# Sums brought to the nodes by products with a stored permutation, in a four-layer graph kernel

## The chip, the cores and the metric

The kernel runs on one core of one Trainium2 chip, in one launch. The metric is device time in microseconds; lower is better. A core has a matrix engine (PE, with its weight loads shown as PEld), a vector engine (DVE), a scalar engine (ACT), a general engine (POOL), a sync engine (SP) that issues transfers, and 16 DMA engines that all queues share. Each engine works through its own queue in order; between engines, semaphores order the work.

## The reference

`x` is 16 graphs of 1024 nodes with 64 features, `adj` their symmetric 0/1 adjacency, `nodemask` is all true. Four layers follow each other; each ends in a residual addition and a layer normalisation over the features. Layers 0 and 3 are the same function with other weights:

```python
adj_d = _dilate_adj(adj, mask)              # drops some edges of nodes with over 10 neighbours
agg   = sum over (tau, w) in ((.25,.25), (.5,.5), (.75,.25)):
            w * interpolated quantile tau, per node and feature, of x over the node's neighbours
out   = x + agg
y     = (relu(out @ W1 + b1) @ W2 + b2) * mask
x     = layernorm(x + y)
```

Layer 1 is `adj @ (x @ W) + b`, layer 2 is `gelu(((softmax(x W1 W2' x') + adj) @ x) @ G)`, both with the same ending. The quantiles need a sort of each node's neighbours for each of the 64 features, and that is most of the work.

## The kernel before

**Batches and layers.** For each of the 16 graphs (batches) there are two sorting layers, numbered l = 0 (reference layer 0) and l = 1 (reference layer 3). The kernel runs 32 of them in an order made by `layers`: batches 0, 1 and 2 of l = 0 first, then in turn one of l = 1 and one of l = 0, with l = 1 two batches behind, and the rest of l = 1 at the end. A layer's place in this order is n. From n = 2 to 28 the even n are l = 0 and the odd ones l = 1; n = 29, 30 and 31 are l = 1.

**A graph's lists (`graph`, called by `graph_stream`).** For each batch, `neighbours` and `both_ways` compute the thinned adjacency `near`, `order` sorts the nodes by degree and stores the order as a 0/1 matrix times 2048 in float16, `perm` (128 x 8 x 1024; its memory is shared with `nbt` by the tag "turned"), and `lists` (line 1104) turns it into lists: `hidx`, the neighbour numbers of the 128 nodes with the longest lists (the hubs), `idx`, those of the other 896 nodes, in seven tiles of 128 nodes with at most 22, 16, 13, 11, 10, 9 and 8 slots, and the weights `wt` and `hwt`. It also makes, by small products with `perm`, `node` and `hnode` (lines 1182 to 1192): for each place in the order, the number of the node that stands there. Up to five batches' lists are kept (`KEPT`), and graph b waits for the end of layer 1 of batch b - 5.

**Gathers (`fetch_stream`, line 1289, all on POOL).** A layer first gathers hub rows: 60 indirect DMAs into `hrows`, a ring of 8 buffers, each free again when `turn_stream` has transposed it into `cols`. Then come the rows of the short lists: 22 into `rows0`, 29 into `rows1`, 38 into `rows2`, one buffer each. Each indirect DMA fetches one row of 64 features per partition from a DRAM table of the nodes' features.

**Sorting.** `turn_stream` (PE transposes, ACT copies) brings the hub rows into `cols`. `sort_stream` (line 1379, DVE) sorts the long lists there (`long_lists`, which end in `tot`), and then runs a sorting network over each of the three groups of short rows. `turn_stream` turns `tot` into `hagg` (64 x 2 x 64). `pick_stream` (line 1393) weights the sorted rows on ACT and adds them in PSUM on PE, which gives `agg[0..2]` (128 nodes x 1, 2 and 4 tiles x 64). `hagg` and `agg` are the aggregates in the degree order, not in the order of the nodes.

**Bringing the sums home.** `put` (line 1240) is an indirect DMA on POOL that writes one tile of aggregates to the rows of a DRAM table `sums` named by `node` or `hnode`. A layer has two for the hubs (`put_hub`) and seven for the short tiles (`put_short`). For n up to `SOON` = 2 they come before the next layer's gathers (`put_all`); later, the two hub puts come after the next layer's 60 hub gathers, and the 1, 2 and 4 others ahead of its `rows0`, `rows1` and `rows2` gathers. Since `rows1` and `rows2` have one buffer each, each of those gathers needs the sort of the layer before in that group to be done, and the `put` waits for just that ("sorted").

**The middle (`middle_stream`).** For each n in order `last_step` (line 1529) reads `sums` back as `ag`, adds the features, transposes (8 times 128 columns), and applies the two dense layers and the normalisation. For l = 0 it goes on with reference layers 1 and 2 (`spread_layer`, `attention_layer`), both of which multiply by the adjacency with `by_adj` (line 1560): 16 loads of 256 KB into `at`, which has three buffers, each followed by a product of 512 columns. The result `x3` is the table of the layer l = 1 of that batch.

**What sets the order.** The streams are generators. `give_out` (line 211) goes through them with estimated costs and due times, always takes the step that could start first (on a tie, the earlier stream: graph, turn, pick, weight, middle, sort, fetch), and so writes out one fixed order for each engine's queue, the queues of SP and ACT for DMAs among them. `Wait(event)` holds a stream back until another stream has given out the step that sets the event; `.after(t)` adds t ns to the estimated readiness of a step.

Of the kernel before, what the change touches and what calls it, by code (L numbers as in the profile page):

```python
# [41 lines left out]
LAG = 2  # L42
KEPT = LAG + 3
SPARE = max([CH * HC] + [64 * n * s for _, n, s in TILE_GROUPS])
SOON = 2
HROWS = 8


# [735 lines left out]
def listed_path(ctx: ExitStack, tc: tile.TileContext, x, adj, nodemask,  # L784
# [48 lines left out]
    V.tensor_scalar(tie_up, tie, 1.0 / (4 * N), None, ALU.add)  # L833
    key_row = const.tile([1, N], F16, name="key_row")
    G.iota(key_row, pattern=[[1, N]], base=1 - 2048, channel_multiplier=0, allow_small_or_imprecise_dtypes=True)
    node16 = iota([P, NT], F16, [[P, NT]], cm=1, name="node16")

    numbers = const.tile([P, NT, 2 * CH - 1], F16, name="numbers")
    V.memset(numbers, 0.0)
# [242 lines left out]
    def order(op, pso, deg, perm):  # L1082
# [18 lines left out]
        for t in range(NT):  # L1101
            yield V.tensor_scalar(perm[:, t], place, rank[:, t:t + 1], 2048.0, ALU.is_equal, ALU.mult)

    def lists(lp, psl, b, near, perm, deg, k):

        k.idx = kp.tile([P, 7, MOST], U32, name="idx")
        k.hidx = kp.tile([P, 2, NG], U32, name="hidx")
        k.node = kp.tile([P, NT], U32, name="node")
        k.hnode = kp.tile([64, 2], U32, name="hnode")
        k.wt = kp.tile([P, 7, MOST], F32, name="wt")  # L1110
        k.hwt = dram.tile([P, CH, 2 * HC], F16, name="hwt", bufs=KEPT)
        dn = lp.tile([P, 2, NT], F16, name="dn")
        yield V.tensor_copy(dn[:, 0], deg)
        yield V.tensor_copy(dn[:, 1], node16)


        pt = psl.tile([P, NT, P], F32, name="two")
# [58 lines left out]
            yield V.tensor_scalar(k.idx[:, g - 1, :cap], top[:, :cap], 0.0, None, ALU.max)  # L1176
        events.add(("idx", b))

        pd = psl.tile([P, NT, 2], F32, name="one")
        for g in range(NT):  # L1180
            for t in range(NT):
                yield T.matmul(pd[:, g, :], perm[:, t, g * P:(g + 1) * P], dn[:, :, t],
                         start=(t == 0), stop=(t == NT - 1))
        dg = lp.tile([P, NT], F32, name="dg")
        yield V.tensor_scalar(dg, pd[:, :, 0], 1.0 / 2048, None, ALU.mult)
        yield V.tensor_scalar(k.node, pd[:, :, 1], 1.0 / 2048, None, ALU.mult)
        ph = psl.tile([64, 2], F32, name="one")
        for h in range(2):
            for t in range(NT):
                yield T.matmul(ph[:, h:h + 1], perm[:, t, h * 64:(h + 1) * 64], dn[:, 1, t:t + 1],  # L1190
                         start=(t == 0), stop=(t == NT - 1))
        yield V.tensor_scalar(k.hnode, ph, 1.0 / 2048, None, ALU.mult)
        more = lp.tile([P, NT], F32, name="more")
        yield V.tensor_tensor(more, dg, caps, ALU.subtract)
        most = lp.tile([P, 1], F32, name="most")
# [22 lines left out]
        for r in range(4):  # L1218
            hd = lp.tile([P, 8, 2 * HC], F16, name="hd")
            for c0, _, n, k0, chunks, by_list in HUB_RUNS:  # L1220
                cols = slice(c0, c0 + n * chunks)
                names, dim = ("(l k)", 2) if by_list else ("(k l)", 3)
                shape = [P, 8, n, chunks] if by_list else [P, 8, chunks, n]
                yield V.tensor_tensor(hd[:, :, cols].rearrange(f"p s {names} -> p s {names[1:-1]}", k=chunks),
                                      hw[:, k0 * CH:(k0 + chunks) * CH].rearrange("p (k s) -> p s k", k=chunks)
                                      [:, 8 * r:8 * r + 8].unsqueeze(dim).to_broadcast(shape),
                                      my_list[:, cols].rearrange(f"p {names} -> p {names[1:-1]}", k=chunks)
                                      .unsqueeze(1).to_broadcast(shape), ALU.mult)
            ho = lp.tile([P, 8, 2 * HC], F16, name="ho")
            for q in range(2):  # L1230
                pw = psl.tile([P, 8 * HC], F32, name="one")
                yield T.matmul(pw, halves, hd[:, 4 * q:4 * q + 4].rearrange("p s c -> p (s c)"), start=True, stop=True)
                yield A.copy(ho[:, 4 * q:4 * q + 4].rearrange("p s c -> p (s c)"), pw)
            yield A.dma_start(k.hwt[:, 8 * r:8 * r + 8, :], ho)

    def fetched(table, dst, rows):
        return G.indirect_dma_start(out=dst, out_offset=None, in_=table[:, :],
                                    in_offset=bass.IndirectOffsetOnAxis(ap=rows, axis=0))

    def put(sums, rows, src):  # L1240
        return G.indirect_dma_start(out=sums[:, :], out_offset=bass.IndirectOffsetOnAxis(ap=rows, axis=0),
                                    in_=src, in_offset=None)

    def slots_ap(buf, place, f, width):

# [22 lines left out]
        if b >= LAG:  # L1268
            layers.append((1, b - LAG))

    def put_hub(n, k):
        yield Wait("hagg", n)
        yield Wait("sums", n)
        for h in range(2):
            yield put(k.sums, k.hnode[:, h:h + 1], k.hagg[:, h])

    def put_short(n, k, q):
        t0, ntiles, _ = TILE_GROUPS[q]
        yield Wait("sorted", n, q)
        for t in range(ntiles):  # L1280
            yield put(k.sums, k.node[:, t0 + t:t0 + t + 1], k.agg[q][:, t])

    def put_all(n, k):
        yield from put_hub(n, k)
        for q in range(3):
            yield from put_short(n, k, q)
        events.add(("put", n))

    def fetch_stream():
        for n, (l, b) in enumerate(layers):  # L1290
            k = batches[b]
            yield Wait("hidx", b) if l == 0 else Wait("x3", b)
            table = tables[l][b % (2 + l * (LAG - 1))]
            k.hrows = [None] * NG
            last = batches[layers[n - 1][1]] if n else None
            early = n <= SOON
            if n and early:
                yield from put_all(n - 1, last)
            for g in range(NG):
                m = n * NG + g - HROWS  # L1300
                if m >= 0:
                    yield Wait("turned", m // NG, m % NG // 4)
                rows = qp.tile([P, 2, C], F32, name="hrows", bufs=HROWS)
                e = min(P, (2 * HC - g * GC) * CH)
                for h in range(2):
                    yield fetched(table, rows[:e, h, :], k.hidx[:e, h, g:g + 1])
                k.hrows[g] = rows
                events.add(("h", n, g))
            if n and not early:
                yield from put_hub(n - 1, last)  # L1310
            yield Wait("idx", b)
            for q, (t0, ntiles, places) in enumerate(TILE_GROUPS):
                if n and not early:
                    yield from put_short(n - 1, last, q)
                rows = qp.tile([P, places, ntiles, C], F32, name=f"rows{q}")
                for t in range(ntiles):
                    for s in range(TILE_CAPS[t0 - 1 + t]):
                        yield fetched(table, rows[:, s, t, :], k.idx[:, t0 - 1 + t, s:s + 1])
                k.rows[l, q] = rows
                events.add(("rows", n, q))  # L1320
            if n and not early:
                events.add(("put", n - 1))
        yield from put_all(n, batches[layers[-1][1]])

    def turn_stream():
        for n, (l, b) in enumerate(layers):
            k = batches[b]
# [51 lines left out]
    def sort_stream():  # L1379
        for n, (l, b) in enumerate(layers):  # L1380
            k = batches[b]
            yield Wait("cols", n, 0)
            if n > 1:
                yield Wait("put", n - 2)
            k.tot = qp.tile([P, 64], F32, name="tot", bufs=2)
            yield from long_lists(n, k)
            events.add(("hubdone", n))
            for q, (_, ntiles, places) in enumerate(TILE_GROUPS):
                yield Wait("rows", n, q)
                yield from network((k.rows[l, q], spare((places, ntiles, C))), plans[q], C)  # L1390
                events.add(("net", n, q))

    def pick_stream():

        for n, (l, b) in enumerate(layers):
            k = batches[b]
            if n > 1:
                yield Wait("put", n - 2)
            k.agg = []
            for q, (t0, ntiles, _) in enumerate(TILE_GROUPS):  # L1400
                yield Wait("net", n, q)
# [127 lines left out]
    def last_step(n, l, b, k):  # L1529
# [1 line left out]
        w1, b1, w2, b2 = ends[l]  # L1531
        xn = features("xn")
        yield D.dma_start(xn, by_part(x[b] if l == 0 else k.x3[1:, :]))
        yield Wait("put", n)
        ag = features("ag")
        yield D.dma_start(ag, by_part(k.sums)).after(8000)
        yield V.tensor_add(ag, ag, xn).after(5000)
        py = one([P, NT, C])
        yield T.matmul(py, ones_row, b2.unsqueeze(1).to_broadcast([1, NT, C]), start=True, stop=False)
        for h in range(NH):  # L1540
            ts = range(h * (HALF // P), (h + 1) * (HALF // P))
            pt = one([C, HALF])
            for t in ts:
                yield T.transpose(pt[:, t % (HALF // P) * P:(t % (HALF // P) + 1) * P], ag[:, t, :], ident)
            ot = mp.tile([C, HALF], F32, name="ot")
            yield A.copy(ot, pt)
            ph = one([H, HALF])
# [10 lines left out]
        return (yield from layernorm(z, ag, features("y")))  # L1558

    def by_adj(k, xn):  # L1560

# [88 lines left out]
    def middle_stream():  # L1650
        for n, (l, b) in enumerate(layers):
            k = batches[b]
            k.sums = dram.tile([N, C], F32, name="sums", bufs=2)
            events.add(("sums", n))
# [70 lines left out]
```

## Time and profile before

| | us |
|---|---|
| median of three runs | 8264.22 |
| lowest and highest of the three | 8253.03, 8267.44 |
| the profiled execution | 8260.65 |
| its span, first to last instruction | 8258.9 |
| mean granted PE clock, as a share of full speed | 0.739 |

The span is what the profile divides into shares. Its page gives busy time per engine; time in which an engine's queue issues a DMA or waits counts as idle, also on POOL, where each indirect DMA is shown as an instruction of about a microsecond. A line of a group reads: engine, operation, tile written <- tiles read, count, then busy time and mean duration in ns, then the idle time just before these instructions and what ended most of it. Starts of the steady part, read off POOL's first hub gather of each layer: layer 7 starts at 2145.7 us, layer 9 at 2632.3, layer 11 at 3117.2, and so on to layer 27 at 7000.7; layers 28 to 31 start at 7246.6, 7478.0, 7705.5 and 7932.8. Layer 3 starts at 1101.0, layers 0, 1 and 2 at 188.8, 520.0 and 883.8. The last hub gather's layer ends its gathers at 8165.0.

### The profile page before, as it was taken

Reading aid. Unit: us, or ns where it says so; the run is one execution under the profiler, and the core shown is the slowest. Engines: PE = TensorE matmul, PEld = TensorE weight load, DVE = VectorE, ACT = ScalarE, POOL = GpSimd, SP = SyncE. Lnnn points to the kernel's source line nnn. Section 1 sums busy time; section 2 is a strip of 40 time slices with the busy share of each in tenths; the row PEclk is TensorE's granted clock in tenths of the full one; section 3 lists DMA queues with packets and bytes.
Section 4 is the critical chain, followed back from the end, with each engine's and each line's share of the span. In section 5 each row is a group of like instructions: output and inputs, shape, how many; then the busy total and the mean of one; then the engine's idle time right before and its main releaser. Section 6 shows DMA issues by size and latency. Waiting matters only on the chain. (4 is left out here: it accounts for less than half of the span.)

```text
span 8258.9 us, 83245 instructions
## 1 busy us (share of the span) xinstructions
PE 5314.9 (64%) x24947; PEld 2777.2 (34%) x24947; DVE 6878.5 (83%) x14791; ACT 2726.7 (33%) x7346; POOL 5640.8 (68%) x5087
## 2 busy tenths in 40 slices
PE   6568786847657576675857667585766758272542
PEld 4243433333333333333333333333333333131221
DVE  2769688778889888888988888898888889889685
ACT  3333433233242424324242432424233242221221
POOL 0635567657676776767777676777777777777774
PEclk8779877768778686877868677686877769565655
DMA  1322424232332323223232322323242232232311
GB/s 48 70 64 57 95 44 98 44 72 51 68 74 54 79 58 82 50 56 82 57 74 58 86 53 51 80 62 75 51 93 52 52 77 65 33 68 36 66 32 21
DMA packets 761595, 513.79 MB, mean 62 GB/s; under 512 B 458672, under 2 KB 600112, under 8 KB 760880
## 3 DMA queue, kind: packets, MB, share of 16 engines
q1 hardware_dynamic: 457008, 261.89, 13.3%
q0 software_dynamic: 161792, 163.90, 12.5%
q10 hardware_dynamic: 142336, 82.59, 3.3%
q8 instruction: 202, 3.31, 0.2%
q14 instruction: 257, 2.11, 0.1%
HBM read 408.64 MB, written 103.55 MB: 62 GB/s over the span
## 5 line engine op out<-in xcount | busy, mean ns | idle before, releaser
L180 POOL DMA_INDIRECT rows<-table,idx x2848 | 3247.0, 1140 | 868.0 <-issue 840.3
L180 POOL DMA_INDIRECT hrows<-table,hidx x1920 | 2054.8, 1070 | 1069.3 <-issue 457.2
L180 DVE TENSOR_TENSOR spare<-cols 128x528 f32<-128x528 f32 (+11 forms) x1632 | 1058.9, 675 | 74.6 <-ACT cols L180 49.1
L180 DVE TENSOR_TENSOR cols<-spare 128x528 f32<-128x528 f32 (+11 forms) x1664 | 1073.2, 681 | 14.8
L180 PE MATMUL turned<-ident,hrows 128*128 128x128 f32 x960 | 348.2, 394 | 936.8 <-DMA hrows<-table,hidx 663.1
L180 PE MATMUL picked<-rows,ident 128*128 128x64 f32 (+2 forms) x2496 | 676.0, 388 | 399.8 <-ACT rows L180 398.9
L180 PEld LDWEIGHTS picked<-rows,ident 128*128 128x128 f32 x2496 | 500.8, 259 | 557.9 <-ACT rows L180 483.3
L180 POOL DMA_INDIRECT sums<-agg,node x224 | 261.3, 1166 | 559.1 <-DMA sums<-agg,node 175.3
L180 ACT ACTIVATE rows<-rows,wt 128x64 f32<-128x64 f32 x2272 | 608.4, 340 | 104.2 <-DVE rows L180 104.2
L180 DVE TENSOR_TENSOR spare<-rows 128x64 f32<-128x64 f32 (+8 forms) x1056 | 542.4, 543 | 80.9 <-DMA hrows<-table,hidx 25.1
L180 PE MATMUL two<-run,nbt 128*128 128x512 f16 (+3 forms) x1536 | 426.4, 452 | 238.0 <-ACT v L180 238.0
L180 PEld LDWEIGHTS turned<-ident,hrows 128*128 128x128 f32 x960 | 169.7, 185 | 1197.2 <-issue 713.3
L180 PE MATMUL pi<-hot,numbers 128*32 128x236 f16 x4096 | 521.1, 273 | 70.1 <-DVE hot L180 66.1
L180 PEld LDWEIGHTS <-nbt 128*128 128x128 f16 x3584 | 310.6, 115 | 670.8 <-issue 610.7
L180 PE MATMUL two<-near,perm 128*128 128x512 f16 x1792 | 507.0, 434 | 0.0
L180 PEld LDWEIGHTS <-numbers 128*32 128x32 f16 x4096 | 382.4, 99 | 335.9 <-issue 291.1
L180 DVE TENSOR_TENSOR spare<-spare 128x944 f32<-128x944 f32 (+11 forms) x672 | 451.2, 671 | 19.1
L180 DVE TENSOR_TENSOR rows<-spare 128x512 f32<-128x512 f32 (+9 forms) x896 | 459.2, 538 | 1.3
L180 ACT COPY cols<-turned 128x512 f32<-128x512 f32 (+3 forms) x288 | 149.2, 529 | 870.9 <-PE turned L180 867.9
L180 PE MATMUL one<-xt,wt 64*128 64x512 f32 x512 | 356.7, 821 | 62.8 <-DVE top L180 62.7
L180 DVE TENSOR_TENSOR spare<-cols,spare 128x472 f32<-128x472 f32 (+2 forms) x704 | 380.9, 541 | 14.7
L180 DVE TENSOR_TENSOR rows<-rows,spare 128x64 f32<-128x64 f32 (+4 forms) x1120 | 364.8, 331 | 19.2
(238 smaller groups left out, 10048.0 us busy)
## 6 DMA issues: line engine op xcount, KB each, us to landing
at<-adjt SPq DMA_DIRECT2D x512, 256.0 KB
a<-in_adj_dram SPq DMA_DIRECT2D x128, 512.0 KB
adjt<-at ACTq DMA_DIRECT2D x128, 512.0 KB
rows<-table,idx POOLq DMA_INDIRECT x2848
hrows<-table,hidx POOLq DMA_INDIRECT x1920
hw<-hwt SPq DMA_DIRECT2D x64, 472.0 KB
hwt<-ho ACTq DMA_DIRECT2D x64, 236.0 KB
ag<-sums SPq DMA_DIRECT2D x32, 256.0 KB
```

Of the source, the lines that this page charges most:

```text
L180: return Step(lambda: f(*args, **kw), self.engine, cost, late, reads, writes, "dma" in name)
```

## The change

The puts, `node`, `hnode`, `sums` and `SOON` are gone. `lists` ends in a new function, `turned_order`: it transposes `perm` back on PE (64 blocks of 128 x 128 in float16), scales it to 0/1 in float32 on ACT, and stores it from ACT's queue as `back` in DRAM, 4 MB a graph. In `last_step` the sums are not read back: for each half of 512 nodes the aggregates are multiplied by the matching rows of `back` (two products with `hagg`, seven with `agg`), which adds every aggregate to its node's column in one PSUM tile, transposed as the dense layer needs it; each of the nine products has its own load into `at`, the tile with three buffers that `by_adj` uses too. The features are added by four more products with the identity, in place of DVE's addition and the transposes. `rows0` gets a second buffer, so that its gathers need the sort of the layer before the last one only. `tot`, `hagg` and `agg`, which waited for the event "put" of layer n - 2, wait for "used", which is set when the products of that layer have been given out.

```diff
+    def turned_order(lp, psl, perm, k):
+
+        k.back = dram.tile([NH, N, HALF], F32, name="back", bufs=KEPT)
+        for g in range(NT):
+            pb = psl.tile([P, NT, P], F16, name="one")
+            for t in range(NT):
+                yield T.transpose(pb[:, t, :], perm[:, t, g * P:(g + 1) * P], ident16)
+            back = lp.tile([P, N], F32, name="rest", bufs=2)
+            yield A.activation(back, pb.rearrange("p t n -> p (t n)"), AF.Copy, scale=1.0 / 2048)
+            yield A.dma_start(k.back[:, g * P:(g + 1) * P, :].rearrange("h r n -> r h n"),
+                              back.rearrange("r (h n) -> r h n", h=NH))
...
     def lists(lp, psl, b, near, perm, deg, k):
-        k.node = kp.tile([P, NT], U32, name="node")
-        k.hnode = kp.tile([64, 2], U32, name="hnode")
...
-        yield V.tensor_scalar(k.node, pd[:, :, 1], 1.0 / 2048, None, ALU.mult)
-        ph = psl.tile([64, 2], F32, name="one")
-        for h in range(2):
-            for t in range(NT):
-                yield T.matmul(ph[:, h:h + 1], perm[:, t, h * 64:(h + 1) * 64], dn[:, 1, t:t + 1],
-                         start=(t == 0), stop=(t == NT - 1))
-        yield V.tensor_scalar(k.hnode, ph, 1.0 / 2048, None, ALU.mult)
...
+        yield from turned_order(lp, psl, perm, k)
...
     def fetch_stream():
...
-            if n and early:
-                yield from put_all(n - 1, last)
...
-            if n and not early:
-                yield from put_hub(n - 1, last)
             yield Wait("idx", b)
             for q, (t0, ntiles, places) in enumerate(TILE_GROUPS):
-                if n and not early:
-                    yield from put_short(n - 1, last, q)
-                rows = qp.tile([P, places, ntiles, C], F32, name=f"rows{q}")
+                if n > (q == 0):
+                    yield Wait("sorted", n - 1 - (q == 0), q)
+                rows = qp.tile([P, places, ntiles, C], F32, name=f"rows{q}", bufs=1 + (q == 0))
...
     (sort_stream and pick_stream)
-                yield Wait("put", n - 2)
+                yield Wait("used", n - 2)
...
     def last_step(n, l, b, k):
-        yield Wait("put", n)
-        ag = features("ag")
-        yield D.dma_start(ag, by_part(k.sums)).after(8000)
-        yield V.tensor_add(ag, ag, xn).after(5000)
+        yield Wait("hagg", n)
+        for q in range(3):
+            yield Wait("sorted", n, q)
...
             pt = one([C, HALF])
+            for g in range(NT + 1):
+                at = mp.tile([P, HALF], F32, name="at", bufs=3)
+                if g < 2:
+                    yield D.dma_start(at[:64], k.back[h, g * 64:(g + 1) * 64, :])
+                    yield T.matmul(pt, k.hagg[:, g], at[:64], start=(g == 0), stop=False)
+                else:
+                    q = sum(t0 < g for t0, _, _ in TILE_GROUPS) - 1
+                    yield D.dma_start(at, k.back[h, (g - 1) * P:g * P, :])
+                    yield T.matmul(pt, k.agg[q][:, g - 1 - TILE_GROUPS[q][0]], at, start=False, stop=False)
             for t in ts:
-                yield T.transpose(pt[:, t % (HALF // P) * P:(t % (HALF // P) + 1) * P], ag[:, t, :], ident)
+                c0 = t % (HALF // P) * P
+                yield T.matmul(pt[:, c0:c0 + P], xn[:, t, :], ident, start=False, stop=(t == ts[-1]))
+            if h == NH - 1:
+                events.add(("used", n))
```

More of the change, by code (lines that the diff above doesn't have):

```diff
@@ L44 @@
 SPARE = max([CH * HC] + [64 * n * s for _, n, s in TILE_GROUPS])
-SOON = 2
 HROWS = 8
@@ L835, in listed_path @@
     G.iota(key_row, pattern=[[1, N]], base=1 - 2048, channel_multiplier=0, allow_small_or_imprecise_dtypes=True)
-    node16 = iota([P, NT], F16, [[P, NT]], cm=1, name="node16")
     numbers = const.tile([P, NT, 2 * CH - 1], F16, name="numbers")
@@ L1107, in lists @@
         k.hidx = kp.tile([P, 2, NG], U32, name="hidx")
-        k.node = kp.tile([P, NT], U32, name="node")
-        k.hnode = kp.tile([64, 2], U32, name="hnode")
         k.wt = kp.tile([P, 7, MOST], F32, name="wt")
         k.hwt = dram.tile([P, CH, 2 * HC], F16, name="hwt", bufs=KEPT)
-        dn = lp.tile([P, 2, NT], F16, name="dn")
-        yield V.tensor_copy(dn[:, 0], deg)
-        yield V.tensor_copy(dn[:, 1], node16)
+        d16 = lp.tile([P, NT], F16, name="d16")
+        yield V.tensor_copy(d16, deg)
         pt = psl.tile([P, NT, P], F32, name="two")
@@ L1177, in lists @@
         events.add(("idx", b))
-        pd = psl.tile([P, NT, 2], F32, name="one")
+        pd = psl.tile([P, NT], F32, name="one")
         for g in range(NT):
             for t in range(NT):
-                yield T.matmul(pd[:, g, :], perm[:, t, g * P:(g + 1) * P], dn[:, :, t],
+                yield T.matmul(pd[:, g:g + 1], perm[:, t, g * P:(g + 1) * P], d16[:, t:t + 1],
                          start=(t == 0), stop=(t == NT - 1))
         dg = lp.tile([P, NT], F32, name="dg")
-        yield V.tensor_scalar(dg, pd[:, :, 0], 1.0 / 2048, None, ALU.mult)
-        yield V.tensor_scalar(k.node, pd[:, :, 1], 1.0 / 2048, None, ALU.mult)
-        ph = psl.tile([64, 2], F32, name="one")
-        for h in range(2):
-            for t in range(NT):
-                yield T.matmul(ph[:, h:h + 1], perm[:, t, h * 64:(h + 1) * 64], dn[:, 1, t:t + 1],
-                         start=(t == 0), stop=(t == NT - 1))
-        yield V.tensor_scalar(k.hnode, ph, 1.0 / 2048, None, ALU.mult)
+        yield V.tensor_scalar(dg, pd, 1.0 / 2048, None, ALU.mult)
         more = lp.tile([P, NT], F32, name="more")
@@ L1238, in fetched @@
                                     in_offset=bass.IndirectOffsetOnAxis(ap=rows, axis=0))
-    def put(sums, rows, src):
-        return G.indirect_dma_start(out=sums[:, :], out_offset=bass.IndirectOffsetOnAxis(ap=rows, axis=0),
-                                    in_=src, in_offset=None)
     def slots_ap(buf, place, f, width):
@@ L1269, in listed_path @@
             layers.append((1, b - LAG))
[L1271 to L1287, printed above, removed]
     def fetch_stream():
@@ L1294, in fetch_stream @@
             k.hrows = [None] * NG
-            last = batches[layers[n - 1][1]] if n else None
-            early = n <= SOON
-            if n and early:
-                yield from put_all(n - 1, last)
             for g in range(NG):
@@ L1320, in fetch_stream @@
                 events.add(("rows", n, q))
-            if n and not early:
-                events.add(("put", n - 1))
-        yield from put_all(n, batches[layers[-1][1]])
     def turn_stream():
@@ L1397, in pick_stream @@
             if n > 1:
-                yield Wait("put", n - 2)
+                yield Wait("used", n - 2)
             k.agg = []
@@ L1557, in last_step @@
         yield V.tensor_add(z, z, xn).after(6000)
-        return (yield from layernorm(z, ag, features("y")))
+        return (yield from layernorm(z, features("ag"), features("y")))
     def by_adj(k, xn):
@@ L1652, in middle_stream @@
             k = batches[b]
-            k.sums = dram.tile([N, C], F32, name="sums", bufs=2)
-            events.add(("sums", n))
             y = yield from last_step(n, l, b, k)
```

## The prediction

> **What bounds the kernel now.** Every instruction carries line 180, the helper that records it, so I go by tiles. I read four views in this order: the page's busy sums, the busy times in windows cut at the first hub gather of every second layer, the POOL groups and timeline inside those windows, and then the waits of DVE and PE.
>
> ```profile
> PE 5314.9 (64%) x24947; PEld 2777.2 (34%) x24947; DVE 6878.5 (83%) x14791; ACT 2726.7 (33%) x7346; POOL 5640.8 (68%) x5087
> ```
> ```profile
> 4573.80:5061.60 487.80, 332.83 (x1573) 172.73 (x1572) 430.73 (x928) 172.66 (x464) 354.34 (x316) 0.76 0.31 66
> 5061.60:5546.60 485.00, 330.51 (x1557) 174.11 (x1557) 427.71 (x922) 169.15 (x458) 354.36 (x316) 0.75 0.32 66
> ...
> 7478.00:7705.50 227.50, 57.81 (x187) 40.12 (x187) 190.89 (x399) 41.84 (x158) 171.86 (x159) 0.50 0.22 34
> ```
> (Window and its length, busy us and instructions of PE, PEld, DVE, ACT, POOL, then granted clock, DMA share, GB/s.) By the busy sums DVE is the bound and POOL has a third to spare. The windows correct this. From 2145.7 to 7000.7 us there are ten equal pairs of layers (one of each kind, with one graph), 485.5 us each; DVE is busy 428 of them, PE 329, POOL 353 in 316 or 317 transfers. But a POOL transfer is not 1.12 us: each is followed by 0.30 us of issue.
>
> ```profile
> 4674.33 0.92 POOL L180 DMA_INDIRECT hrows<-table,hidx  x1 [0.30 <-issue]
> 4675.55 0.92 POOL L180 DMA_INDIRECT sums<-hagg,hnode  x1 [0.30 <-ACT ag L180]
> 4677.91 1.00 POOL L180 DMA_INDIRECT sums<-hagg,hnode  x1 [1.44 <-DMA sums<-hagg,hnode]
> 4680.79 0.97 POOL L180 DMA_INDIRECT sums<-agg,node  x1 [1.88 <-DVE rows L180]
> 4682.07 1.53 POOL L180 DMA_INDIRECT rows<-table,idx  x1 [0.30 <-issue]
> ```
> The POOL groups between 2145 and 7000 us (busy, mean ns | idle before):
> ```profile
> L180 POOL DMA_INDIRECT rows<-table,idx x1781 | 2034.7, 1142 | 542.8 <-issue 533.6 <-DMA rows<-table,idx 5.2 <-PE pi L180 2.4
> L180 POOL DMA_INDIRECT hrows<-table,hidx x1200 | 1289.9, 1075 | 519.7 <-issue 285.0 <-PE turned L180 161.3 <-DMA hrows<-table,hidx 53.3
> L180 POOL DMA_INDIRECT sums<-agg,node x140 | 167.6, 1197 | 214.8 <-DMA sums<-agg,node 106.0 <-DVE spare L180 25.6 <-DVE nb L180 21.6
> L180 POOL DMA_INDIRECT sums<-hagg,hnode x40 | 42.2, 1055 | 44.7 <-DMA sums<-hagg,hnode 38.6 <-issue 3.0 <-ACT ag L180 2.7
> ```
> Busy and idle of these four lines add to 4856 of 4855 us: POOL's queue is never without work, and only 161 us of it waits for another engine (the hub gathers for a free place). So **POOL is the bound**, and the puts hold it 167.6 + 42.2 + 214.8 + 44.7 = 469 us in ten pairs, 47 a pair, half of it because one put waits for the one before it to land. DVE waits next to never for gathered rows (2.8 us in the ten pairs); the bound reaches it through PE, whose queue stands behind turns that wait for hub rows (waits of PE, then of DVE, 4573 to 5061 us):
>
> ```profile
> PE turned L180 <- DMA hrows<-table,hidx: 43.0, 27, 6.7
> PE turned L180 <- ACT cols L180: 19.5, 3, 12.1
> ...
> PE turned L180 <- DVE tot L180: 12.2, 2, 6.5
> ```
> ```profile
> DVE deg L180 <- ACT near L180: 10.9, 1, 10.9
> DVE z L180 <- ACT z L180: 9.5, 2, 8.8
> ```
>
> **What it removes.** All 288 puts, the `sums` table with its write and read, and on DVE one 0.68 us addition a layer and three copies of about 0.16 us a graph. POOL's own work for a pair falls to (4856 - 469 - 161) / 10 = 422 us. DVE's falls to 428 - 1.4 - 0.5 = 426, and its gaps under 150 ns (3204 in the ten pairs, 112 us by the time stamps) make that 437. So **DVE's 437 is the next floor**, before any wait.
>
> **What it adds to PE.** Per layer, 18 products of 512 columns in float32. The nearest row is the adjacency product, which loads its operand the same way: two passes, 1.07 us.
> ```profile
> 3422.99 1.07 PE L180 MATMUL po<-at,y 128*64 128x512 f32 x2
> ```
> 36 x 1.07 = 38.5 us a pair. Eight transposes a layer become products of the same 128 columns in two passes (+0.11 us each, +2 a pair); 64 f16 transposes a graph at 108.1 us / 1024 (the row one<-ident,nb) are 6.8; 16 tiny products go (-0.5). Together +47: PE goes from 329 to 376 of the pair. Bounds: the passes start 0.43 us apart, so 31 us at least for the 36; 36 x 1.07 plus the mean load pace below at most.
>
> [...]
>
> **What it adds to the queues.** SP: 18 loads a layer (4.2 MB) through three `at` buffers. The adjacency product runs the same loop at 16 products in 3417.5 to 3460.2 us, 2.4 us a load, so 18 take about 43 us plus a first landing of some 4. What they replace took 35 us in layer 10 (ag<-sums issued 3320.3, the addition done 3355.7). The serial chain of the middle stream, 2349 to 2740 us for a pair (391), becomes about 391 + 2 x 12 = 415. It starts earlier by the wait for the last put (agg copied at 3756, the read of the sums at 3805: 49 us). Behind these loads on SP stand the hw loads (due at `summed`), the next graph's `a` and the write of x3; the gathers of a layer come 434 us after its x3 (3170, 3604), so that cover is wide. ACT: eight copies of 1.01 us and eight 512 KB writes a graph, on an engine busy 172 of 486; I cost them at nothing there, and at 8 us if that cover failed. DMA: 8.4 MB of loads and 4.2 MB of writes a pair on top of 66 GB/s x 485 us = 32 MB; a share of 0.31 becomes about 0.41. No cost.
>
> **What it moves.** In the first layers nothing is gained: the hub gathers of layers 1 and 2 start at 520 and 884, but their lists (hidx) are ready only at 497 and 832, and the graph grows by eight rounds of transposes, copy and write in two buffers (2 to 4 us a round by the same rows) before `perm`'s memory is free: 16 to 34 us later for each graph. I take 0 for everything before 1101 us (-40 to +50). The waits on the event "put" become waits on "used"; for an odd layer "used" of n-2 comes the middle part of an even layer (3320 to 3654, 334 us) + 12 + 47 of loads = 393 us after the sort of n-3, the sort of n starts a full pair after it: free while a pair is above 393. rows1 and rows2 still wait for the sort of the layer before, as the puts ahead of them did.
>
> **The pair.** Floors: POOL 422, DVE 437, middle 415, PE 376 plus its waits. PE idles 485 - 329 = 156 now, of which 43 + 20 + 12 (shown above) are lateness of POOL and DVE; without them PE needs 376 + 81 = 457. DVE idles 46 a pair beyond its small gaps; about half is the deg and z kind that ends with late hub rows, half its own back-and-forth with ACT: 437 + 23 = 460. Both ways give **460**, bounds 437 and 483.
>
> **The sum.** Ten pairs: -255 (-485 to -25). 1101 to 2145.7 us: two pairs in 1044.7, DVE busy 875 of it: -70 (-140 to 0). 7000.7 to 8165.3: five layers without a graph at 233 us, DVE 175 to 219, POOL less 23.5: -21 each, -105. The end: the last agg lands at 8202.5 and ag is complete at 8215.7; now ten or so loads and products follow it: +12 (0 to +25). Together -418: 8259 - 418 = 7841 of span. The profiled execution took 8260.65 and the median of the runs shown is 8264.22, so I state **7840**, its own range 7700 to 7980.
>
> **Rivals.** (1) DVE alone decides: with POOL and the hub rows ahead, its waits nearly vanish and a pair is 442. For it: DVE's order holds sort work at nearly every moment. Against: waits such as ln_v, top and rs are its own. -435 - 100 - 115 + 0 gives 7610. (2) A new wait takes the old one's place: the middle stream, 415 of floor with DVE steps in it that queue behind a fuller DVE, or rows1 and rows2 waiting for the sort; a pair of 475 gives -105 - 30 - 80 + 25, so 8070. (3) Slower: PE becomes the bound. The 36 products stand in one in-order queue with the turns, picks and graph; if each added load wait there only replaces a wait for hub rows, the idle 156 stays and a pair is 329 + 47 + 156 = 532; twelve pairs at +47, the last layers still -105, the start +50, give about 8770. It decides as soon as PE's idle stays above 485 - 376 = 109 a pair. Against it: the adjacency loop costs PE only 3 us of load waits in a pair. (4) The gains and losses cancel within what this measurement can tell, 0.2% (17 us).
>
> The Trainium skill's page "SBUF — State Buffer" (Who interferes with whom) adds a cost I leave out of the sum: a two-input DVE operation contends with a POOL instruction that reads SBUF. The trace fits (of 3160 transfers, none of the 211 beside an idle DVE took over 1.25 us, 351 of 1154 beside a sort step into `spare` did); a fuller DVE would lengthen those 211 by an estimated 20 us in ten pairs.
>
> **Chances.** My forecast 0.50, rival 1 0.15, rival 2 0.22, rival 3 0.10, rival 4 0.03. Faster by over 0.2%: 0.87; within: 0.03; slower: 0.10. The range, 7590 to 8120, takes in both faster rivals and leaves out most of rival 3 and the lower part of rival 1.
>
> **What would show it.** No put on POOL; pairs near 460; POOL waiting for DVE (hrows behind turned, rows behind the pick) by 30 to 40 us a pair; DVE busy over 90% of a pair; PE's waits for hub rows well under 43. Wrong if PE's idle per pair stays near 150, if DVE waits for ACT or PE for more than 46 a pair, or if SP's loads make the products wait more than a few us.

## The result: slower by 9%, and the profile after

| | before | changed |
|---|---|---|
| median, us (four runs each) | 8261.85 | 9036.91 |
| lowest and highest | 8253.03, 8267.44 | 8992.10, 9046.84 |
| profiled execution, its span | 8260.65, 8258.9 | 9046.31, 9044.3 |

The changed kernel takes 1.0929 of the time before, interval 1.0889 to 1.0968. At times the kernel before itself took 9521 to 9719 us (9521 and 8260 on one and the same chip), and one changed kernel (g3 and h1 below) then read 1.033 of it in place of 1.006, from a cause that was not found; so every ratio below is to a run of the kernel before on the same chip at the same time, and sizes and conclusions rest on the runs beside one of about 8260. Each kernel of the experiments ran once; the four runs of the changed kernel lie within 0.6%.

First the busy sums of the changed kernel's page and its two POOL groups, over the whole span.

```profile
PE 6116.5 (68%) x27123; PEld 2958.6 (33%) x27123; DVE 6814.0 (75%) x14711; ACT 2863.4 (32%) x7474; POOL 5238.5 (58%) x4798
...
L179 POOL DMA_INDIRECT rows<-table,idx x2848 | 3264.5, 1146 | 1896.6 <-PE picked L179 1037.9
L179 POOL DMA_INDIRECT hrows<-table,hidx x1920 | 1968.0, 1025 | 1774.8 <-PE turned L179 813.1
```

DVE and POOL have less work than before, PE more, and none is nearer to full but PE. A gather still takes 1.03 to 1.15 us. But POOL now waits 1038 + 813 us for PE; over its whole span the kernel before waited 316 us for PE's turns and never over 0.3 us at a time for its picks. (Picks are PE's products into the tile `picked`, turns its transposes into `turned`.) The windows put the loss in place: the ten pairs from layer 7 to 27, then the rest, in the kernel before and in the changed one (columns as in the prediction).

```profile
2145.70:7000.70 4855.00, 3288.42 (x15604) 1722.71 (x15603) 4280.16 (x9231) 1705.11 (x4597) 3533.34 (x3161) 0.76 0.31 66
7000.70:8258.90 1258.20, 515.51 (x1371) 261.87 (x1370) 1001.23 (x2128) 285.85 (x966) 878.57 (x799) 0.58 0.23 43
```
```profile
2123.70:7665.50 5541.80, 3906.89 (x16975) 1852.66 (x16974) 4228.48 (x9154) 1789.40 (x4672) 3262.99 (x2980) 0.75 0.33 79
7665.50:9044.30 1378.80, 674.54 (x1945) 291.59 (x1943) 1020.81 (x2190) 296.13 (x979) 809.05 (x745) 0.65 0.28 61
```

A pair went from 485.5 to 554.2 us: 687 of the 785 us are lost there, 121 at the end, and 22 gained at the start. PE works 62 us a pair more and still idles 5542 - 3907 = 1635 us, 163 a pair. The waits of POOL, PE and DVE in the changed kernel's ten pairs (us in total, times, longest):

```profile
POOL rows L179 <- PE picked L179: 837.3, 23, 55.8
POOL hrows L179 <- PE turned L179: 559.5, 63, 61.5
...
PE turned L179 <- DMA hrows<-table,hidx: 687.6, 346, 4.8
...
DVE z L179 <- PE one L179: 258.8, 9, 43.5
DVE top L179 <- PE two L179: 167.4, 34, 34.8
DVE hd L179 <- PE one L179: 156.5, 19, 29.5
```

POOL waits for PE's picks and turns, PE for POOL's hub rows, DVE for PE: three engines wait for each other in a ring. One turn of it, in the timeline of the changed kernel around 4611 to 4767 us:

```profile
4611.79 0.94 POOL L179 DMA_INDIRECT hrows<-table,hidx  x1 [0.30 <-issue]
4635.21 0.94 POOL L179 DMA_INDIRECT hrows<-table,hidx  x1 [22.47 <-PE turned L179]
...
4665.88 0.45 PE L179 MATMUL turned<-ident,hrows 128*128 128x128 f32 x1 [1.53 <-DMA hrows<-table,hidx]
4668.28 0.45 PE L179 MATMUL turned<-ident,hrows 128*128 128x128 f32 x1 [1.96 <-DMA hrows<-table,hidx]
...
4693.53 0.25 PE L179 MATMUL turned<-ident,hrows 64*128 64x64 f32 x1 [1.71 <-DMA hrows<-table,hidx]
...
4695.18 0.53 PE L179 MATMUL picked<-rows,ident 128*128 128x64 f32 x2
...
4706.02 0.69 DVE L179 TENSOR_TENSOR z<-one,y 128x512 f32<-128x512 f32 x1 [42.91 <-PE one L179]
...
4766.61 1.37 POOL L179 DMA_INDIRECT rows<-table,idx  x1 [45.99 <-PE picked L179]
```

POOL stands 22 us for a place among the hub rows. When it goes on, PE has reached the turns of those rows in its queue and takes them one by one, 1.6 to 3.3 us apart, as they land (18 us of PE's time from 4662 to 4706 us are such waits). Between and behind the turns, in the same queue, stand products of the middle stream; DVE, whose next instruction is the `z` that needs the last of them, sits for 43 us and sorts nothing. So the sort is late, the pick after it is late, and the gather that needs the picked rows' buffer waits 46 us, which makes the next hub rows late.

### The profile page after: what moved, and what is told of

Read it like the earlier page. It is cut to its first block, busy times and chain, and to the rows that moved or that the text cites. A ratio compares the mean times of both kernels' runs of the same rounds, so it can differ in the third digit from the quotient of the medians.

```text
span 9044.3 us, 88574 instructions
## 1 busy us (share of the span) xinstructions
PE 6116.5 (68%) x27123; PEld 2958.6 (33%) x27123; DVE 6814.0 (75%) x14711; ACT 2863.4 (32%) x7474; POOL 5238.5 (58%) x4798
## 4 chain that ended last, share of the span: by engine, by line
DVE 23%; PE 12%; DMA 8%; POOL 8%; issue 5%; ACT 3%; SPq 0%; DVEq 0%; POOLq 0%; ACTq 0%
DVE spare L179 9%; PE one L179 6%; DVE cols L179 6%; DMA hrows<-table,hidx 5%; POOL hrows L179 4%; POOL rows L179 4%; PE two L179 4%; DVE rows L179 3%; DVE hot L179 2%; DVE top L179 1%; DMA at<-back 1%; PE po L179 1%; PE picked L179 1%; DMA a<-in_adj_dram 1%; DMA at<-adjt 1%
## 5 line engine op out<-in xcount | busy, mean ns | idle before, releaser
L179 POOL DMA_INDIRECT hrows<-table,hidx x1920 | 1968.0, 1025 | 1774.8 <-PE turned L179 813.1
L179 ACT ACTIVATE rows<-rows,wt 128x64 f32<-128x64 f32 x2272 | 630.4, 341 | 152.5 <-DVE rows L179 143.0
L179 PE MATMUL one<-at,agg 128*64 128x512 f32 x896 | 565.2, 738 | 107.4 <-DMA at<-back 106.0
L179 PE MATMUL two<-near,perm 128*128 128x512 f16 x1792 | 528.2, 448 | 0.0
L179 PE MATMUL two<-run,nbt 128*128 128x512 f16 (+3 forms) x1536 | 394.8, 426 | 110.2 <-ACT v L179 110.2
L179 PEld LDWEIGHTS <-perm 128*128 128x128 f16 x3840 | 298.6, 111 | 455.7 <-issue 341.8
L179 PE MATMUL po<-at,y 128*64 128x512 f32 x512 | 319.7, 725 | 133.8 <-ACT y L179 83.1
```

The source lines that it names most:

```text
L179: return Step(lambda: f(*args, **kw), self.engine, cost, late, reads, writes, "dma" in name)
```

## The experiments

Three theories. **Theory 1**: the added work is the loss, PE's products and their loads (rival 3). **Theory 2**: the order of the queues is the loss; rows and hub rows wait for what frees their buffers because the puts no longer hold the order back. **Theory 3**: the turned order is the loss, by its transposes, stores and the later start of a graph.

**Parts taken out, in the order that the program makes of what is left.** One buffer for `rows0`, with the wait that goes with it; no products and loads; no turned order (the products load `adj` in its place); products without loads, of one constant tile.

```diff
 e1  -  rows = qp.tile([P, places, ntiles, C], F32, name=f"rows{q}", bufs=1 + (q == 0))
     +  rows = qp.tile([P, places, ntiles, C], F32, name=f"rows{q}")
 e2  -  for g in range(NT + 1):
     -      at = mp.tile([P, HALF], F32, name="at", bufs=3)
...
 e3  -  yield from turned_order(lp, psl, perm, k)
...
     -  yield D.dma_start(at, k.back[h, (g - 1) * P:g * P, :])
     +  yield D.dma_start(at, adj[b, (g - 1) * P:g * P, h * HALF:(h + 1) * HALF])
 e4  -  at = mp.tile([P, HALF], F32, name="at", bufs=3)
     +  at = still
```

> The changed kernel with one buffer for rows0 again. If the added work on PE is what costs (theory 1), the second buffer matters little: 9000 to 9080 us. If it is the queue order, POOL's head blocked by rows1 while PE waits for hub rows (theory 2), moving POOL's gathers moves the time by more than 1% one way or the other, below 8950 or above 9130. If the permutation turned back for each graph costs (theory 3), 9000 to 9080.

> The changed kernel without the 18 products a layer and their loads; the aggregates are left out of the result, the rest and all waits stay. Theory 1 (PE's added work): PE loses 38 us of a pair, and the time falls below before, 7800 to 8100. Theory 2 (order of the queues): no puts and no products, but the same loop of waits, 8500 to 9000. Theory 3 (turning the permutation back): 8700 to 9000.

> The changed kernel without the permutation turned back and stored; the products load rows of the adjacency of the same size in its place, so the aggregates go to wrong nodes. Theory 3: most of the loss goes, 8200 to 8500. Theory 1: PE loses 7 us of a pair, 8900 to 9000. Theory 2: 8700 to 9100.

> The changed kernel with its products but without their loads: a constant tile of zeros stands in, so the aggregates are left out of the result. Theory 1 by PE's work alone: stays at 8900 to 9050. Theory 1 by waits for the loads in PE's queue: 8100 to 8400. Theory 2: 8500 to 9000, since the order around the hub rows stays.

Measured, against 9521.42 us before: e1 10539.80 (1.107), e2 10337.69 (1.086), e3 10864.31 (1.141), e4 10672.26 (1.121). The changed kernel itself was not run beside them, so the expectations in us cannot be held against them and single sizes cannot be read. Taking out a part did not bring any of them near the kernel before. What all four share with the change is that the puts are gone, and, counted in their traces as in the table below, its order: PE has 29.6 to 30.0 of the 30 turns ahead of a layer's first pick. They give a hint and no proof.

That leads to the order. `give_out` estimates when each step could start and always gives out the earliest. It knows what a step reads and when that was written. It does not know that a new tile lies in the buffer of an older one: each tile has a name of its own. A gather into `rows1` reads only the table and `idx`, so for `give_out` it can start long before its buffer is free. In the kernel before, a put stood ahead of it on POOL, and the put reads `agg`, the result of the sort; so POOL's estimated clock came to the sort before the gather was placed. Without the put nothing holds it back, the hub rows of the next layer seem to be there early, and their turns are placed early in PE's queue.

**The order alone, both ways.** f1 is the whole change; the first gather into each rows tile also names, for `give_out` only, the aggregate whose sort frees the buffer. f2 is the kernel before with the puts' reads hidden from `give_out`, those of the two hub puts in the same way. In both the work on the chip is the same as without the edit, instruction for instruction by operation and tile; c1 is the changed kernel, run beside them, and f3 is f1 with the loads into `at` told of their three buffers too.

```diff
 f1  -  yield fetched(table, rows[:, s, t, :], k.idx[:, t0 - 1 + t, s:s + 1])
     +  step = fetched(table, rows[:, s, t, :], k.idx[:, t0 - 1 + t, s:s + 1])
     +  if t == s == 0 and n > (q == 0):
     +      step.reads.append(batches[layers[n - 1 - (q == 0)][1]].agg[q].tensor.name)
     +  yield step
 f2  -  yield put(k.sums, k.node[:, t0 + t:t0 + t + 1], k.agg[q][:, t])
     +  step = put(k.sums, k.node[:, t0 + t:t0 + t + 1], k.agg[q][:, t])
     +  step.reads.clear()
     +  yield step
```

> The changed kernel unaltered, as the yardstick for the runs beside it on the same chip. All theories: 1.08 to 1.12 times before.

> The changed kernel; only the order differs. The first gather into each of rows0, rows1 and rows2 tells the order-maker that it comes after the aggregate whose copy frees the buffer, as the puts told it before; no work and no wait of the chip's is added. Theory 2 in its sharper form (without the puts nothing in the written order holds POOL's gathers back to when their buffers are free, so PE's turns of hub rows are placed too early and block its queue): at least 7% less than the changed kernel, 0.93 to 1.03 of before. Theory 1 (PE's added work): within 2% of the changed kernel, 1.07 to 1.12 of before.

> The kernel before, with its puts and sums; only the order differs. The puts no longer tell the order-maker which aggregates they read, so the order is written as if POOL never had to wait for the sort. Theory 2: slower than before by 4% or more, 1.04 to 1.12, with PE's turns waiting for hub rows much longer. Theory 1: same work, same time, 0.99 to 1.01 of before.

> As f1_rows_told, and each load into the tile of three buffers, in the products and in the adjacency products, also tells the order-maker that it waits for the product three loads earlier. Theory 2: as f1 or up to 3% better, if the loads misplaced in the queues of PE and SP cost too; if the order now written is only slower for the middle stream, up to 2% worse. Theory 1: 1.06 to 1.12 of before.

Measured, against 8254.69: c1 9040.32 (1.095), f1 8305.43 (1.006), f2 9160.78 (1.110), f3 8369.16 (1.014). A read named for the order alone, three to a layer, gives back 735 us of the change's 786, and hiding the puts' reads in the kernel before costs it 906. f3 is 64 us slower than f1: telling the loads too did not help. POOL's and DVE's waits of f2 in its ten pairs, then POOL's of f1:

```profile
POOL sums L180 <- ACT rows L180: 503.7, 16, 55.9
POOL hrows L180 <- PE turned L180: 279.2, 65, 21.9
...
DVE ln_v L180 <- ACT ag L180: 547.3, 20, 51.9
DVE ag L180 <- DMA ag<-sums: 274.8, 10, 31.3
```
```profile
POOL hrows L179 <- PE turned L179: 538.3, 59, 61.9
...
POOL rows L179 <- PE picked L179: 206.3, 17, 29.3
```

In f2 the ring shuts in another place: POOL's puts wait 504 us for ACT's weighting of the sorted rows, DVE waits 275 us for sums that POOL has not brought, and 547 us for ACT. In f1 the 837 us for the pick are down to 206, and DVE's `z` waits for PE of 259 us to 31; POOL's waits for PE's turns stay (560 and 538). The order can be counted in the traces: of the 30 turns of the next layer's hub rows, how many PE has to do ahead of a layer's first pick (mean over layers 8 to 27):

| | even layers | odd layers | a pair, us |
|---|---|---|---|
| before | 23.0 | 14.4 | 485.5 |
| changed | 30.0 | 29.6 | 554.2 |
| f2 | 30.0 | 30.0 | 555.3 |
| f1 | 26.7 | 16.5 | 495.5 |
| f3 | 17.8 | 26.1 | 503.8 |
| h1 (below) | 25.7 | 10.8 | 500.5 |
| h2 (below) | 22.3 | 15.8 | 485.2 |

Theory 2 is shown for the loss: the order alone, with no change of work, makes 735 of the 786 us in the changed kernel and 906 us in the kernel before. That the early turns are the part of the order that does it is read from the ring and from this table, where the two slow kernels have all 30 ahead in nearly every layer; no run moved the turns and nothing else.

**More told, and parts taken out of the mended order.** f5 is the change and f6 the kernel before, with `give_out` told of every buffer of the streams: `BEFORE` names, for each tile, the one that had its buffer. f7 is f1 without the products and loads, f8 is f1 without the turned order.

```diff
 f5, f6   for w in h.writes:
              ready = max(ready, read.get(w, 0.0))
     +        if w in BEFORE:
     +            ready = max(ready, read.get(BEFORE[w], 0.0))
```

> The changed kernel; only the order differs, as in f1_rows_told, but now every buffer of a pool on the chip tells the order-maker that it is free only when the tile before in it has been read. If the rest of the loss in f1 (1.006 of before) comes from other buffers that the order does not know (hub rows, cols, the tile of three loads, PSUM), 0.94 to 0.99 of before. If it comes from the work that the change adds, 1.00 to 1.03.

> The kernel before with every buffer told in the same way; its puts stay. If POOL's queue is its floor whatever the order, 0.99 to 1.02 of before. If before too loses to its order, under 0.99.

> f1_rows_told without the 18 products a layer and their loads; the aggregates are left out of the result. If the added products are what is left of the loss, 0.94 to 0.98 of before; if the order of the graph's steps is, 0.99 to 1.01.

> f1_rows_told without the permutation turned back and stored; the products load rows of the adjacency instead, so the aggregates go to wrong nodes. If turning it back is what is left of the loss, 0.95 to 0.98 of before; if not, 0.99 to 1.02.

Measured, against 9682.45: f5 9957.29 (1.028), f6 9634.54 (0.995), f7 9691.77 (1.001), f8 10263.09 (1.060). f1 was not run beside them, so whether telling everything helps more than telling the rows stays open; f5's order puts 10.0 and 0.6 turns ahead of the first pick, fewer than the kernel before. f8 lies above both of its ranges, and f7, without products, is not below the kernel before. Whether the turned order costs anything is not settled: f8 was not run beside a kernel before of about 8260.

**What keeps the mended change from a gain.** Four kernels in six runs: f1 again (g1), f7 again (g2 and h2), the gathers held back just as the puts were, to `hagg` and to the sort of the layer before (g3 and h1), and that with ten buffers for hub rows (g4).

```diff
 g3, h1  -  if n > (q == 0):
         -      yield Wait("sorted", n - 1 - (q == 0), q)
         +  if n:
         +      yield Wait("hagg", n - 1)
         +      yield Wait("sorted", n - 1, q)
...
         +      last = batches[layers[n - 1][1]]
         +      step.reads.extend([last.hagg.tensor.name, last.agg[q].tensor.name])
 g4      -  HROWS = 8
         +  HROWS = 10
```

> The changed kernel with the first gather into each rows tile held back in the order to the sort that frees its buffer, a second time. Theory 2 (the order alone loses the time): 0.99 to 1.02 of the kernel before on any chip. If the earlier 1.006 was a matter of that one chip: 1.04 or more here.

> The order held back as in the run before it, and the nine products and loads for each half left out (the aggregates are not added). If PE's added products (38 us a pair by the prediction) are what keeps the change from a gain once the order is mended: 0.96 to 0.98 of the kernel before, pairs of 465 to 480 us. If what is left of the order's waits decides: within 0.01 of the run with the products.

> The changed kernel whose gathers into each group of rows are held back in the order just as the puts ahead of them were: to hagg and to the sort of the layer before, for rows0 too. All the work of the change is in it. If the anchor that the puts gave, whole, is what the order needs: under 0.99 of the kernel before (pairs of 460 to 480 us). If the second buffer of rows0 is worth using: slower than the run with rows alone told (over 1.006). PE as the bound: 1.00 to 1.03 whatever is told.

> The run before this one, with ten buffers for hub rows in place of eight. If POOL's waits for a free place among the hub rows (575 us in ten pairs where the rows were told) are on the path: 20 to 40 us a pair shorter, 0.95 to 0.97. If they only take the place of other waits: within 0.01 of it.

> The whole change with the gathers held back in the order as the puts were, once more. On a chip where the kernel before takes about 8260 us: under 0.995 of it if the whole anchor was what the order still lacked when only the rows were told (1.006); 1.00 to 1.01 if it was not. On a chip where it takes over 9500 us: 1.03, as in the run before.

> The mended order of the rows alone, without the nine products and loads for each half. Where the kernel before takes about 8260 us: 0.96 to 0.98 of it if the products (38 us a pair) are what eats the gain; 1.00 to 1.01 if the order's remaining waits do. Where it takes over 9500 us: 1.00 to 1.015, as in the two runs before.

Measured, against 9718.77: g1 10220.49 (1.052), g2 9853.38 (1.014), g3 10040.69 (1.033), g4 10031.66 (1.032). Against 8260.24: h1 8311.36 (1.006), h2 8087.15 (0.979). g1 missed what theory 2 expected, 0.99 to 1.02, and g2 lies in neither of its ranges; h1, the kernel of g3 again but beside 8260, is at 1.006, so a mended order reads 1.006 on a second chip too. Holding the gathers back just as before is no better than telling the rows (h1 and f1 agree within 6 us). Two more places for hub rows moved g4 by 9 us from g3, beside 9719 alone. h2 without the products takes 8305 - 8087 = 218 us less than f1, whose rule for the order it has. So the products with their loads keep the mended change from a gain; but leaving them out also shifts the order that is written (26.7 turns ahead in even layers become 22.3, as in the table), and how much of the 218 us is that shift was not tested.

But even h2, without products, gains only 173 us. Its two windows and POOL's waits in the ten pairs:

```profile
2088.20:6940.60 4852.40, 3450.96 (x16603) 1827.13 (x16601) 4231.46 (x9100) 1767.85 (x4613) 3352.57 (x2981) 0.76 0.31 72
6940.60:8085.40 1144.80, 483.29 (x1503) 249.26 (x1501) 999.73 (x2158) 292.18 (x975) 816.61 (x745) 0.60 0.24 48
```
```profile
POOL rows L179 <- PE picked L179: 314.9, 18, 36.8
POOL hrows L179 <- PE turned L179: 294.8, 42, 36.7
```

A pair is 485.2, as before (485.5), with 469 us of puts gone from POOL's ten pairs. Its waits for PE are now 315 + 295 = 610 us, against 161 before; 161 + 469 = 630. This fits puts that stood in time that POOL would have waited anyway; but h2 also holds the turned order, which adds work on PE and ACT, and no run beside 8260 left out both. All of h2's gain lies outside the pairs: 57 us before layer 7 and 113 after layer 27.

## Why the prediction was wrong

It said 7840, faster with 0.87; it is 9037. The spans, against the sum on record, by its own stretches (each kernel less the kernel before, us):

| | predicted | changed | f1 | h1 | h2 |
|---|---|---|---|---|---|
| up to layer 7 | -70 | -22 | -23 | -28 | -57 |
| ten pairs | -255 | +687 | +100 | +150 | -3 |
| from layer 27 | -105 + 12 | +121 | -33 | -71 | -113 |
| together | -418 | +785 | +45 | +50 | -174 |

**The step that failed** is the one on moved waits: "rows1 and rows2 still wait for the sort of the layer before, as the puts ahead of them did." On the chip they do. In `give_out` they do not: there only the put knew of the sort. Removing an instruction removed an edge from the program that writes the order, and the order was rewritten as a whole. The prediction treated the order as given and costed the edit at nothing; it costs 735 us (c1 less f1). The front part of the document even names the rule (`give_out` takes the step that could start first); what was not asked is what it can see of a step that no longer has a put ahead of it.

**"So POOL is the bound"** failed too, and hid behind the first. The reading was that busy and idle of POOL's four lines fill its time and only 161 us wait for another engine. By the releasers that the profile names, another 96 us of waits ahead of the puts are for DVE and ACT, and 145 of the 469 us, not half, for the landing of an earlier put. But the step itself is the fault: an engine that always has something to do is not therefore what the others wait for. h2 removes the puts and a pair does not move. The reading that fits is that POOL was one member of a ring (gather, turn, sort, pick, gather) and its puts were cover; the turned order as what holds h2's pair at 485 is not ruled out. Whether some other order would turn those 47 us a pair into time stays open; three orders tried (f1, f3, h1) did not, with the products, and one without (h2).

**The terms for work.** The sums came out in f1: a pair holds 372 us of PE (376 predicted; 391 in the changed kernel), 423 of DVE (426), and POOL's gathers with their issue take 421 (422).

```profile
2123.00:7078.30 4955.30, 3724.78 (x16968) 1797.52 (x16968) 4226.83 (x9149) 1781.35 (x4670) 3325.12 (x2981) 0.80 0.37 88
```

The products' own term was too small. Their rows in f1, over the whole span:

```profile
L179 PE MATMUL one<-at,agg 128*64 128x512 f32 x896 | 548.2, 718 | 103.4 <-DMA at<-back 102.1
L179 PE MATMUL one<-at,hagg 64*64 64x512 f32 x256 | 196.7, 878 | 60.8 <-DMA at<-back 60.5
```

That is 745 us for 576 products, 1.29 us each and 46.6 a pair, where the sum had 1.07 and 38.5. PE's whole busy sum falls by less, from 5937.6 in f1 to 5416.6 in h2, 521 us: the ends of products overlap with what follows, and the mean granted clock differs (0.80 in f1's ten pairs, 0.76 in h2's), so this difference is no clean price of a product. The 1.07 us is what a product takes at full clock. In the changed kernel two adjacency products of the same form, 5 us apart, show both paces:

```profile
4688.56 1.97 PE L179 MATMUL po<-at,y 128*64 128x512 f32 x2
...
4693.71 1.07 PE L179 MATMUL po<-at,y 128*64 128x512 f32 x2
```

The trace's clock record grants half of full speed at the first and all of it at the second. Of the 1152 passes of f1's products 366 started at half clock. The page "TensorE: Matmul & The Clock Gate" of the Trainium skill (Loop structure matters more than you think) shows a loop with a long DMA wait ahead of every matmul, 8 us in its example, that runs cold, at half clock. The products here, 18 loads in 37 us or more, fit that in part: a third of their passes ran at half clock and two thirds at full.

**Outside the pairs** the mechanism held for single layers and not for the sums. f1's layers 28 to 30 take 210, 213 and 209 us, against 231, 228 and 227 before, 15 to 21 less where 21 was predicted. But its layer 27 takes 294 us against 246, so that the stretch from layer 27 gained 33 us and not 93; and up to layer 7 it gained 23 and not 70.

**What the added loads cost was mis-sized.** Predicted: 47 us a layer from the first load to the last product, +12 over what they replace, and no wait of PE. In f1 it is 40 to 62 us in even layers and 37 to 93 in odd ones, the products standing in PE's queue among other work, and PE waits 8 us a pair for the loads (10 in the changed kernel). With the order mended, leaving out the products and their loads saves 218 us (f1 less h2), where the sum had them nearly free.

**Rivals.** Rival 3 (PE's idle stays) had the right direction and the right thing to look for: 163 us of idle a pair, far above its 109. Its mechanism was wrong: the waits for the added loads are 95 us of the 1635, and f1, with all the products, is 735 us faster. Rival 2 named the right place (rows waiting for the sort) at 475 a pair, where it came to 554. Of the signs listed, all three for "wrong" came true: PE's idle near 150 (163), DVE's waits for ACT and PE above 46 a pair (111), products that wait for their loads (10 us a pair).

## What to carry to other kernels

Where a program writes the order of the queues, list what it can see of each step you remove, data edges and buffer reuse apart: an instruction that looks like pure cost may be the only thing that tells the order when a buffer is free. Test it both ways, by giving the edge back without the instruction and by hiding the edge with the instruction still there. And an engine that is always occupied is the bound only if its work, taken out, is not replaced by waits; look for a ring of waits through in-order queues before counting its busy time as time to gain.

## What the runs showed of the hardware

The trace's clock records hold two values only, 1.0 and 0.5 of full speed. The two passes of an added product (512 columns, float32) start 0.43 to 0.48 us apart in f1 where both began at 1.0, and 0.85 to 0.91 where both began at 0.5. Products of 512 columns in float16 (`two<-near,perm` in the kernel before) mostly start 0.22 and 0.43 us apart. A mean clock says little of one loop: over the ten pairs it rose from 0.76 before to 0.80 in f1, while a third of the products' own passes ran at half.

In the kernel before an indirect write to `sums` takes 1.06 or 1.20 us in the mean (40 and 140 of them in the ten pairs). Where the profile puts the wait ahead of one down to the landing of an earlier one, 75 times, that wait adds 1.9 us in the mean (38.6 us in 20 waits, 106.0 in 55).
